# Half-width coupling products in two of four stages of a recurrence, and input gates spread over both

## The chip, the cores and the metric

The kernel runs on one core of a Trainium2 chip. The metric is the device time of one execution in microseconds, as a median over several runs of the same kernel. Beside the runs stands one profiled execution, whose trace records the instructions of each engine: TensorE (PE for matmuls, PEld for loads of the stationary operand), VectorE (DVE), ScalarE (ACT), GpSimd (POOL) and the queue of SyncE (SP).

## The reference

Four layers act on x of shape (8, 256, 512), each added to x. The first two are attention layers (one masked, one modulated by a condition vector). The last two are recurrences over the 256 time steps, for a batch of 8 and 512 features. The oscillator takes one Runge-Kutta step of four stages for each time step:

```python
def _derivative(q, p, drive, coupling, bias):
    i_couple = jnp.tanh(q) @ coupling.T
    dq = q - q ** 3 / 3.0 - p + drive + i_couple + bias
    dp = EPSILON * (q + ALPHA - BETA * p)
    return (dq, dp)

def _rk4_step(q, p, drive, coupling, bias):
    dq1, dp1 = _derivative(q, p, drive, coupling, bias)
    dq2, dp2 = _derivative(q + 0.5 * DT * dq1, p + 0.5 * DT * dp1, drive, coupling, bias)
    dq3, dp3 = _derivative(q + 0.5 * DT * dq2, p + 0.5 * DT * dp2, drive, coupling, bias)
    dq4, dp4 = _derivative(q + DT * dq3, p + DT * dp3, drive, coupling, bias)
    ...
```

Each of the four derivatives needs a product of tanh(q) (8 x 512) with the coupling matrix (512 x 512), and each depends on the one before. The second recurrence is a GRU over the oscillator's result:

```python
def cell(h, x):
    gi = x @ W_ih + b_ih
    gh = h @ W_hh + b_hh
    i_r, i_z, i_n = jnp.split(gi, 3, axis=-1)
    h_r, h_z, h_n = jnp.split(gh, 3, axis=-1)
    r = jax.nn.sigmoid(i_r + h_r)
    z = jax.nn.sigmoid(i_z + h_z)
    n = jnp.tanh(i_n + r * h_n)
    h_new = (1.0 - z) * n + z * h
    return (h_new, h_new)
```

## The kernel before

The attention layers come first (`attention`, lines 25 to 510) and leave the oscillator's drive, transposed, in x2T. Then `scans` runs both recurrences in one loop over the time steps (line 811), written out by hand: the order in the code is the order on each engine. The GRU runs LAG = 7 steps behind the oscillator, since its input gates are made for TS = 4 time steps at once. So from t = 8 to t = 255 every time step holds four oscillator stages s = 0 to 3 and, spread over them, one GRU step.

States are kept transposed: features lie on partitions, four slices and the batch of 8 along the free axis. One stage of the oscillator is this loop:

- `coupling` (line 695) multiplies tanh(q), as stationary operand of 8 columns, with the coupling matrix, as moving operand. The four column blocks j go to the four 32-row strips of one PSUM tile of 128 columns (ic_ps, two of them, used in turn), over four slices k of the contraction. A matmul in fp32 shows in the profile as two records with a load each.
- A VectorE transpose (line 890) brings half of the columns of that tile back to the state's layout, line 891 adds the linear and cubic part (hq) and so gives half of the new q, and `tanh_half` (line 597, on ScalarE) makes the stationary operand of the next stage from it. Then the same for the other half. The first two slices k of the next coupling need the first half of tanh, the last two the second.
- Beside this, ScalarE squares q (line 836), VectorE makes mm (line 847) and hq (line 851) ahead of the transpose, ScalarE scales copies of q (line 679) and GpSimd adds them to the linear parts W of the later stages (line 693). In stage 3, p and the next step's W follow (lines 844 to 846 and `linear_p`).

The GRU step lies between these:

- `gru_products` (line 729) puts 48 products of h and W_hh behind the coupling of its stage: 8 in stage 1, 20 each in stages 2 and 3 (FILL, line 727). All go to one PSUM tile, pg.
- `gru_1` (line 746), in stage 0, transposes pg (line 748), adds the input gates (line 750), and starts the gates r and z on ScalarE and GpSimd. `gru_2` (line 766), in stage 1, makes the argument of n and its tanh, `gru_3` line 773, and `gru_4` (line 775) writes the new h three times into hz (line 778), which the products of stage 1 wait for, and adds it to the output tile on GpSimd (line 785).
- `input_gates` (line 709) multiplies the four finished time steps of a chunk with W_ih, in three parts over three time steps, each behind the coupling of stage 0; `input_gate_out` (line 720) takes the results out in later stages.
- `keep_warm` (line 797) issues matmuls whose result nobody reads, into a PSUM tile of their own, where TensorE would have nothing else.

Of the kernel before, what the change touches and what calls it, by code (L numbers as in the profile page):

```python
# [8 lines left out]
F32 = mybir.dt.float32  # L9
# [5 lines left out]
P = 128  # L15
B, T, D = 8, 256, 512
NJ = D // P
# [511 lines left out]
def scans(ctx, tc, cst, bias, b_ih, b_hh, x2T, out):  # L529
# [49 lines left out]
    psp = ctx.enter_context(tc.tile_pool(name="s_ps", bufs=1, space=PSUM))  # L579

    def rows(j):
        return slice(32 * j, 32 * j + 32)

    cT_sb, wih_sb, whh_sb = cst["weights"]
# [5 lines left out]
    LAG = 2 * TS - 1  # L590
# [9 lines left out]


    q, tT = condS, cst["tanh"]
    ic_ps = [psp.tile([P, P], F32, name=f"ic{i}") for i in range(2)]

    for t in ic_ps:
        nc.vector.memset(t, 0.0)
# [13 lines left out]

    pg_ps = psp.tile([P, P], F32, name="pg")
    gi_ps = psp.tile([P, 3, P], F32, name="gi")
    idle_ps = psp.tile([P, P], F32, name="idle")


    hqs = psp.tile([P, 2, NJ, B], F32, name="hqs")
# [33 lines left out]
    def state3(hz):  # L660
        return hz.rearrange("p k (g x) -> p k g x", x=40)[:, :, :, 0:B]
# [30 lines left out]
        c = scaled(x, [EQ[s][i] for s in range(i + 1, 4)] + [PQ[i]])  # L692
        nc.gpsimd.tensor_tensor(W[:, i + 1 : 5], W[:, i + 1 : 5], c, ALU.add)  # L693

    def coupling(tT, ps):
        for k in range(NJ):
            for j in range(NJ):
                nc.tensor.matmul(  # L698
                    ps[32 * j : 32 * j + B, :],
                    lhsT=tT[k // HM][:, k % HM, :],  # L700
                    rhs=cT_sb[:, k, j * P : (j + 1) * P],
                    start=(k == 0),
                    stop=(k == NJ - 1),
                )


    INPUTS = (((0, 0, 3), (1, 0, 1)), ((1, 1, 3), (2, 0, 2)), ((2, 2, 3), (3, 0, 3)), ())

    def input_gates(c, part):
        for k, g0, g1 in INPUTS[part]:  # L710
            for j in range(NJ):
                nc.tensor.matmul(  # L712
                    gi_ps[rows(j), g0:g1, :],
                    lhsT=x3T[c][:, k, :],
                    rhs=wih_sb[:, k, g0:g1, j * P : (j + 1) * P],
                    start=(k == 0),
                    stop=(k == NJ - 1),
                )

    def input_gate_out(c, g):  # L720
# [8 lines left out]
    def gru_products(tau, s):  # L729
        for k, g0, g1 in FILL[s]:  # L730
            for g in range(g0, g1):
                for j in range(NJ):
                    nc.tensor.matmul(  # L733
                        pg_ps[rows(j), :],
                        lhsT=hzs[tau % 3][:, k, 32 * g : 32 * g + 32],
                        rhs=whh_sb[:, k, g, j * P : (j + 1) * P],
                        start=((k, g) == (0, 0)),
                        stop=((k, g) == (NJ - 1, 2)),
                    )
# [3 lines left out]
    def of_step(tau):  # L743
        return slice(B * (tau % TS), B * (tau % TS) + B)
# [27 lines left out]
    def gru_3():  # L772
        nc.vector.tensor_mul(hm, tn, gru["z1"])  # L773

    def gru_4(tau):

        hz = hzs[(tau + 1) % 3]
        nc.vector.tensor_tensor(  # L778
            state3(hz),
            hm.unsqueeze(2).to_broadcast([P, NJ, 3, B]),  # L780
            gru["zh"].unsqueeze(2).to_broadcast([P, NJ, 3, B]),
            ALU.add,
        )
        x = x3T[tau // TS][:, :, of_step(tau)]
        nc.gpsimd.tensor_tensor(x, x, hz[:, :, 0:B], ALU.add)
# [8 lines left out]
                o[rows(j)].rearrange("p m n -> p (m n)"),  # L794
            )

    def keep_warm(rounds):

        for k in range(rounds):
            for j in range(NJ):  # L800
                nc.tensor.matmul(
                    idle_ps[32 * j : 32 * j + B, :],
                    lhsT=condS[:, k, :],
                    rhs=cT_sb[:, k, j * P : (j + 1) * P],
                    start=True,
                    stop=True,
                )

    with tc.manual_schedule():
        made = []  # L810
        for t in range(T + LAG + 1):
            osc = t < T
            tau = t - LAG
            prod, cell = 0 <= tau < T, 1 <= tau <= T
            inp = TS <= t < T + TS
            c, part = t // TS - 1, t % TS
            if osc:
                if t % TS == 0:
                    x3T[t // TS] = chp.tile([P, NJ, 32], F32, tag="x3T", name=f"x3T_{t // TS}")
                qs = q  # L820
            for s in range(4):
                n = f"{t}_{s}"
                ic = ic_ps[s % 2]

                if osc:
                    coupling(tT, ic)
                if inp and s == 0:
                    input_gates(c, part)
                if t < T + LAG and (not prod or s == 0) and not (inp and s == 0 and INPUTS[part]):
                    keep_warm(2)  # L830
                if not osc and t < T + LAG and s == 3:
                    keep_warm(2)

                if osc:
                    sq, mm, hq = sqmm[:, 0, s % 2], sqmm[:, 1, s % 2], hqs[:, s % 2]
                    nc.scalar.activation(sq, qs, AF.Square, scale=math.sqrt(CUB[s]))  # L836
                if cell and s == 0:
                    gru_1(tau - 1)
                if cell and s == 1:
                    gru_2(tau - 1)  # L840

                if osc:
                    if s == 3:
                        stt(W[:, 4], qs, PQ[3], W[:, 4], ALU.mult, ALU.add)
                        p = st.tile([P, NJ, B], F32, tag="p", name=f"p_{t}")
                        nc.vector.tensor_scalar(p, W[:, 4], CLAMP - OFF, -CLAMP - OFF, ALU.min, ALU.max)  # L846
                    stt(mm, sq, LIN[s], qs, ALU.subtract, ALU.mult)  # L847
                if cell and s == 1:
                    gru_3()
                if osc:  # L850
                    nc.vector.tensor_sub(hq, W[:, s], mm)  # L851
                if cell and s == 1:
                    gru_4(tau - 1)
                if prod:
                    gru_products(tau, s)
                if osc:
                    if s < 3:
                        take(s, qs)
                    if s == 2 and t // US_CH + 1 < T // US_CH:
                        drive(t // US_CH + 1, t % US_CH // NJ, t % NJ)  # L860
                    if t == 0 and s < 3:

                        for i in range(*((0, 5), (5, 10), (10, 16))[s]):
                            drive(0, i // NJ, i % NJ)
                    if 0 < t < TS and s > 0:
                        gru_init(3 * t - 3 + s - 1)
                    if t == TS and s == 1:
                        gru_init(9)
                    if s == 3 and t + 1 < T:
                        W_next = linear_p(t + 1, p)  # L870

                if s == 3:

                    now, made = made, []
                    if cell and (tau - 1) % TS == TS - 1:
                        made.append((tau - 1) // TS)
                    if not osc:
                        now, made = now + made, []
                    for x in now:
                        write_out(x)  # L880
                if inp and (part, s) in ((2, 2), (2, 3), (3, 2)):
                    input_gate_out(c, {(2, 2): 0, (2, 3): 1, (3, 2): 2}[part, s])

                if osc:
                    qn = tmp.tile([P, NJ, B], F32, tag="qn", name=f"qn_{n}", bufs=4)
                    tTn = []
                    for half in range(2):
                        m2 = slice(half * HM, (half + 1) * HM)
                        icT = tmp.tile([P, HM, 32], F32, tag=f"icT{half}", name=f"icT{half}_{n}", bufs=2)
                        nc.vector.transpose(icT.rearrange("p m n -> p (m n)"), ic[:, half * 64 : half * 64 + 64])  # L890
                        stt(qn[:, m2, :], icT[:, :, 0:B], IC[s], hq[:, m2, :], ALU.mult, ALU.add)  # L891
                        if s < 3 or t + 1 < T:

                            tTn.append(tanh_half(qn, half, n))
                    tT = tTn
                    qs = qn
            if osc:
                q = st.tile([P, NJ, B], F32, tag="q", name=f"q_{t}")
                nc.gpsimd.tensor_scalar(q, qs, CLAMP, -CLAMP, ALU.min, ALU.max)
                if t + 1 < T:  # L900
                    W = W_next
                x = x3T[t // TS][:, :, of_step(t)]
                nc.gpsimd.tensor_tensor(x, x2T[:, :, :, t], q, ALU.add)  # L903
# [3 lines left out]
def tile_kernel(  # L907
# [50 lines left out]
    with ExitStack() as s:  # L958
        scans(s, tc, cst, bias, b_ih, b_hh, x2T, out)
# [42 lines left out]
```

## Time and profile before

| | us |
|---|---|
| median of 3 runs | 3043.76 |
| lowest and highest | 3042.32, 3047.22 |
| the profiled execution | 3040.15 |
| its span, first to last instruction | 3038.4 |

The page gives the busy time of each engine over the span, and the costliest groups of instructions; the groups that the change is about are these (line, engine, operation, tiles, shapes, count, then busy us and mean ns of one, then the idle time of the engine before them and what ended most of it):

```profile
PE 2847.2 (94%) x70330; PEld 2070.0 (68%) x70330; DVE 2002.5 (66%) x9090; ACT 1599.9 (53%) x8347; POOL 986.8 (32%) x2905
...
L698 PE MATMUL ic<-cT_sb,tT 128*8 128x128 f32 x32736 | 1088.6, 273 | 82.2 <-ACT tT L598 44.6
L698 PEld LDWEIGHTS ic<-cT_sb,tT 128*8 128x8 f32 x32736 | 758.6, 89 | 344.0 <-ACT tT L598 272.0
L733 PE MATMUL pg<-whh_sb,hz 128*32 128x128 f32 x24576 | 818.5, 274 | 50.7 <-DVE hz L778 17.5
```

Records of one engine overlap: a coupling of 32 records of 273 ns takes 1.06 us from the first start to the last end. A busy time is therefore no sum of costs; what a stage costs is read from the starts in the timeline.

### The profile page before, as it was taken

The page shows a single profiled execution, that of the slowest core. Times are in us where ns is not written, and L with a number is a line of the kernel's source. Part 1 is how long each engine was busy: PE and PEld are TensorE (multiplying, and loading weights), DVE is VectorE, ACT ScalarE, POOL GpSimd, SP SyncE. Part 2 cuts the span into 40 slices and gives each one's busy share as a digit, 9 for nine tenths or more (in the row PEclk, how much of TensorE's full clock was granted, in tenths as well). Part 3 has the DMA queues.
Part 4 walks back from the last instruction along what each step waited for, and adds up shares of the span by engine and source line. Part 5 has one row for each costly group of instructions (what it writes and reads, how often), then busy time and mean ns, then how long its engine had stood idle before and what let it go on. Part 6 is the DMA issues. An engine that isn't in the chain of part 4 may idle for free.

```text
span 3038.4 us, 165918 instructions
## 1 busy us (share of the span) xinstructions
PE 2847.2 (94%) x70330; PEld 2070.0 (68%) x70330; DVE 2002.5 (66%) x9090; ACT 1599.9 (53%) x8347; POOL 986.8 (32%) x2905
## 2 busy tenths in 40 slices
PE   8999999999988899999999999999999999999997
PEld 5455555555545677777777777777777777777775
DVE  4444444544434677777777777777777777777774
ACT  2333433433433566666666666666666666666652
POOL 0021111111221344444444444444444444444442
PEclk8999999999999999999999999999999999999999
DMA  3000000000040000000000000000000000000000
GB/s 129 5 1 1 12 11 1 12 11 1 2 98 2 4 7 6 7 6 6 7 6 7 6 6 7 6 7 6 6 7 6 7 6 6 7 6 7 6 6 7
DMA packets 17759, 35.31 MB, mean 12 GB/s; under 512 B 2144, under 2 KB 10860, under 8 KB 17012
## 3 DMA queue, kind: packets, MB, share of 16 engines
q1 hardware_dynamic: 17012, 24.69, 3.0%
q8 instruction: 550, 9.01, 1.2%
q14 instruction: 197, 1.61, 0.2%
HBM read 20.49 MB, written 4.19 MB: 8 GB/s over the span
## 4 chain that ended last, share of the span: by engine, by line
PE 62%; DVE 26%; ACT 6%; issue 4%; POOL 2%; ACTq 0%; DMA 0%; SPq 0%; POOLq 0%; DVEq 0%
PE pg L733 19%; PE ic L698 17%; PE psqkv L301 5%; DVE icT L890 5%; PE pc L153 5%; DVE qn L891 5%; ACT tT L598 4%; DVE hqs L851 3%; PE s L226 3%; DVE own L748 3%; DVE sqmm L847 2%; PE n L204 2%; DVE v L750 2%; PE psx L401 2%; DVE mxp L209 2%
## 5 line engine op out<-in xcount | busy, mean ns | idle before, releaser
L698 PE MATMUL ic<-cT_sb,tT 128*8 128x128 f32 x32736 | 1088.6, 273 | 82.2 <-ACT tT L598 44.6
L698 PEld LDWEIGHTS ic<-cT_sb,tT 128*8 128x8 f32 x32736 | 758.6, 89 | 344.0 <-ACT tT L598 272.0
L733 PE MATMUL pg<-whh_sb,hz 128*32 128x128 f32 x24576 | 818.5, 274 | 50.7 <-DVE hz L778 17.5
L598 ACT ACTIVATE tT<-qn 128x16 f32<-128x16 f32 x2046 | 440.2, 216 | 646.0 <-DVE qn L891 567.5
L733 PEld LDWEIGHTS pg<-whh_sb,hz 128*32 128x32 f32 x24576 | 667.4, 110 | 125.0 <-DVE hz L778 124.8
L890 DVE STREAM_TRANSPOSE icT<-ic 128x64 f32<-128x64 f32 x2048 | 503.7, 246 | 70.5 <-PE ic L698 64.9
L891 DVE SCALAR_TENSOR_TENSOR qn<-icT,hqs 128x16 f32<-128x16 f32 x2048 | 350.4, 171 | 70.1
L693 POOL TENSOR_TENSOR W<-W,cx 128x128 f32<-128x128 f32 x765 | 297.2, 389 | 256.7 <-ACT cx L679 256.7
L686 POOL TENSOR_TENSOR W<-cx,us 128x128 f32<-128x128 f32 x255 | 117.1, 459 | 446.1 <-ACT cx L679 446.1
L847 DVE SCALAR_TENSOR_TENSOR sqmm<-sqmm,qn 128x32 f32<-128x32 f32 x768 | 153.5, 200 | 152.2 <-ACT sqmm L836 123.1
L209 DVE TENSOR_REDUCE mxp<-n 128x1 f32<-128x512 f32 x256 | 158.7, 683 | 132.0 <-PE n L204 132.0
L851 DVE TENSOR_TENSOR hqs<-W,sqmm 128x32 f32<-128x32 f32 x1020 | 200.1, 196 | 46.1 <-DVE own L773 1.0
L238 ACT ACTIVATE ex<-s 128x512 f32<-128x512 f32 x256 | 132.1, 603 | 157.0 <-PE s L231 157.0
L712 PE MATMUL gi<-wih_sb,x3T 128*32 128x384 f32 (+2 forms) x3072 | 202.4, 379 | 0.5 <-POOL x3T L903 0.5
L324 POOL TENSOR_SCALAR r<-s 128x16 f32<-128x16 f32 x32 | 6.5, 204 | 604.0 <-DVE s L322 603.7
L679 ACT ACTIVATE cx<-qn 128x32 f32<-128x32 f32 x1280 | 200.9, 213 | 0.1
L301 PE MATMUL psqkv<-wqkv_sb,xnT 128*128 128x512 f32 x384 | 181.8, 620 | 0.0
L679 ACT ACTIVATE cx<-p 128x32 f32<-128x32 f32 x1020 | 149.8, 217 | 32.2 <-DVE p L846 1.4
L356 DVE TENSOR_REDUCE mxp<-n 128x2 f32<-128x512 f32 x128 | 79.6, 685 | 107.7 <-PE n L348 107.7
L226 PE MATMUL s<-qm 32*128 32x256 f32 x1024 | 139.4, 406 | 6.8 <-DVE mxp L209 6.8
L679 ACT ACTIVATE cx<-q 128x32 f32<-128x32 f32 x1020 | 145.5, 213 | 0.0
L748 DVE STREAM_TRANSPOSE own<-pg 128x128 f32<-128x128 f32 x256 | 84.9, 332 | 91.3 <-PE pg L733 91.3
(149 smaller groups left out, 3593.5 us busy)
## 6 DMA issues: line engine op xcount, KB each, us to landing
x<-in_x SPq DMA_DIRECT2D x8, 512.0 KB
out<-o SPq DMA_DIRECT2D x256, 16.0 KB
wqkv_sb<-in_L_cond_W_qkv SPq DMA_DIRECT2D x1, 3072.0 KB
wih_sb<-in_L_cond_W_ih SPq DMA_DIRECT2D x4, 768.0 KB
whh_sb<-in_L_cond_W_hh SPq DMA_DIRECT2D x4, 768.0 KB
mk<-in_cond SPq DMA_DIRECT2D x8, 256.0 KB
wemb<-in_L_cond_W_emb SPq DMA_DIRECT2D x4, 512.0 KB
wout_sb<-in_L_cond_W_out SPq DMA_DIRECT2D x1, 1024.0 KB
```

What stands on the lines that cost most here:

```text
L209: nc.vector.tensor_reduce(mxp0[e][:, qc, 32 * h + 1 : 32 * h + 2], ss[h], AX.X, ALU.max)
L226: nc.tensor.matmul(ss[h][:, i, :], lhsT=qm[r : r + 32, e, kc], rhs=qm[r : r + 32, e, qs], start=True, stop=False)
L301: nc.tensor.matmul(ps, lhsT=xnTs[b][:, c, m * P : (m + 1) * P], rhs=wqkv_sb[:, c, part * D : (part + 1) * D], start=(c == 0), stop=(c == N ...
L598: nc.scalar.activation(tT, src[:, half * HM : (half + 1) * HM, :], AF.Tanh)
L679: nc.scalar.activation(c[:, i], x, AF.Copy, scale=f)
L693: nc.gpsimd.tensor_tensor(W[:, i + 1 : 5], W[:, i + 1 : 5], c, ALU.add)
L698: nc.tensor.matmul(ps[32 * j : 32 * j + B, :], lhsT=tT[k // HM][:, k % HM, :], rhs=cT_sb[:, k, j * P : (j + 1) * P], start=(k == 0), stop= ...
L733: nc.tensor.matmul(pg_ps[rows(j), :], lhsT=hzs[tau % 3][:, k, 32 * g : 32 * g + 32], rhs=whh_sb[:, k, g, j * P : (j + 1) * P], start=((k, ...
L847: stt(mm, sq, LIN[s], qs, ALU.subtract, ALU.mult)
L851: nc.vector.tensor_sub(hq, W[:, s], mm)
L890: nc.vector.transpose(icT.rearrange("p m n -> p (m n)"), ic[:, half * 64 : half * 64 + 64])
L891: stt(qn[:, m2, :], icT[:, :, 0:B], IC[s], hq[:, m2, :], ALU.mult, ALU.add)
```

## The change

Four edits, all in `scans`:

1. In stages 0 and 1 a coupling product has 64 columns instead of 128, so that there are 32 matmuls instead of 16. They come in the order AHEAD, (slice k, half): (0,0), (1,0), (0,1), (2,0), (3,0), (1,1), (2,1), (3,1). The halves lie in two PSUM tiles, and three tiles ic_ps are used instead of two (BANKS gives the tile of each stage and half). Stages 2 and 3 keep the whole width and order.
2. `keep_warm` loses its own PSUM tile and writes to that of the three which its stage doesn't use (SPARE).
3. The input gates of each part are divided: most of them stay in stage 0, four matmuls of 128 columns go behind the coupling of stage 1.
4. Where the oscillator runs, `gru_4` and the GRU products of stage 1 are issued between the first transpose of stage 1 and the addition behind it, instead of ahead of that transpose. On VectorE this moves line 778 behind line 890; on GpSimd it moves line 785 behind line 693 of stage 1; on TensorE the order stays.

```diff
-    ic_ps = [psp.tile([P, P], F32, name=f"ic{i}") for i in range(2)]
+    ic_ps = [psp.tile([P, P], F32, name=f"ic{i}") for i in range(3)]
+
+    BANKS = ((0, 1), (2, 0), (1, 1), (2, 2))
+    SPARE = (2, 1, 0, 1)
...
-    idle_ps = psp.tile([P, P], F32, name="idle")
...
-    def coupling(tT, ps):
-        for k in range(NJ):
+    WHOLE = tuple((k, None) for k in range(NJ))
+    AHEAD = ((0, 0), (1, 0), (0, 1), (2, 0), (3, 0), (1, 1), (2, 1), (3, 1))
+
+    def coupling(tT, s):
+        for k, half in AHEAD if s < 2 else WHOLE:
+            n0, n1 = (0, P) if half is None else (64 * half, 64 * half + 64)
+            ps = ic_ps[BANKS[s][half or 0]]
             for j in range(NJ):
                 nc.tensor.matmul(
-                    ps[32 * j : 32 * j + B, :],
+                    ps[32 * j : 32 * j + B, n0:n1],
                     lhsT=tT[k // HM][:, k % HM, :],
-                    rhs=cT_sb[:, k, j * P : (j + 1) * P],
+                    rhs=cT_sb[:, k, j * P + n0 : j * P + n1],
                     start=(k == 0),
                     stop=(k == NJ - 1),
                 )
...
-    INPUTS = (((0, 0, 3), (1, 0, 1)), ((1, 1, 3), (2, 0, 2)), ((2, 2, 3), (3, 0, 3)), ())
-
-    def input_gates(c, part):
-        for k, g0, g1 in INPUTS[part]:
+    INPUTS = (
+        (((0, 0, 3),), ((1, 0, 1),)),
+        (((1, 1, 3), (2, 0, 1)), ((2, 1, 2),)),
+        (((2, 2, 3), (3, 0, 2)), ((3, 2, 3),)),
+        ((), ()),
+    )
+
+    def input_gates(c, units):
+        for k, g0, g1 in units:
...
-    def keep_warm(rounds):
+    def keep_warm(rounds, s):
...
-                    idle_ps[32 * j : 32 * j + B, :],
+                    ic_ps[SPARE[s]][32 * j : 32 * j + B, :],
...
-                if inp and s == 0:
-                    input_gates(c, part)
-                if t < T + LAG and (not prod or s == 0) and not (inp and s == 0 and INPUTS[part]):
-                    keep_warm(2)
+                    coupling(tT, s)
+                units = INPUTS[part][s] if inp and s < 2 else ()
+                input_gates(c, units)
+                if t < T + LAG and (not prod or s == 0) and not units:
+                    keep_warm(2, s)
...
-                if cell and s == 1:
+                if cell and s == 1 and not osc:
                     gru_4(tau - 1)
-                if prod:
+                if prod and not (osc and s == 1):
                     gru_products(tau, s)
...
+                        ic = ic_ps[BANKS[s][half]]
                         nc.vector.transpose(icT.rearrange("p m n -> p (m n)"), ic[:, half * 64 : half * 64 + 64])
+                        if s == 1 and half == 0:
+
+                            if cell:
+                                gru_4(tau - 1)
+                            if prod:
+                                gru_products(tau, s)
                         stt(qn[:, m2, :], icT[:, :, 0:B], IC[s], hq[:, m2, :], ALU.mult, ALU.add)
```

More of the change, by code (lines that the diff above doesn't have):

```diff
@@ L716, in input_gates @@
                     start=(k == 0),
-                    stop=(k == NJ - 1),
+                    stop=((k, g1) == (NJ - 1, 3)),
                 )
@@ L822, in scans @@
                 n = f"{t}_{s}"
-                ic = ic_ps[s % 2]
                 if osc:
-                    coupling(tT, ic)
-                if inp and s == 0:
-                    input_gates(c, part)
-                if t < T + LAG and (not prod or s == 0) and not (inp and s == 0 and INPUTS[part]):
-                    keep_warm(2)
+                    coupling(tT, s)
[3 more added lines that the diff above has]
+                    keep_warm(2, s)
                 if not osc and t < T + LAG and s == 3:
-                    keep_warm(2)
+                    keep_warm(2, s)
                 if osc:
```

## The prediction

> **What bounds the kernel now.** I read the page first. The table of slices shows that the two recurrences fill about two thirds of the span (from 964 us, the first coupling product in the timeline, to 2988 us) at full TensorE clock. The chain that ended last names what decides there:
>
> ```profile
> PE 62%; DVE 26%; ACT 6%; issue 4%; POOL 2%; ACTq 0%; DMA 0%; SPq 0%; POOLq 0%; DVEq 0%
> PE pg L733 19%; PE ic L698 17%; PE psqkv L301 5%; DVE icT L890 5%; PE pc L153 5%; DVE qn L891 5%; ACT tT L598 4%; DVE hqs L851 3%; PE s L226 3%; DVE own L748 3%; DVE sqmm L847 2%; PE n L204 2%; DVE v L750 2%; PE psx L401 2%; DVE mxp L209 2%
> ```
>
> The coupling (L698), the GRU products (L733) and the short loop icT, qn, tT carry it. Then the timeline of one time step, from the last products of stage 3 to the start of stage 2 (start us, length, engine, line, operation, count):
>
> ```profile
> 2006.35 1.27 PE L733 MATMUL pg<-whh_sb,hz 128*32 128x128 f32 x40
> 2007.44 1.06 PE L698 MATMUL ic<-cT_sb,tT 128*8 128x128 f32 x32
> 2007.69 0.33 DVE L748 STREAM_TRANSPOSE own<-pg 128x128 f32<-128x128 f32 x1 [0.27 <-PE pg L733]
> 2008.06 0.26 DVE L750 TENSOR_TENSOR v<-own,gis 128x96 f32<-128x96 f32 x1
> 2008.23 0.19 DVE L847 SCALAR_TENSOR_TENSOR sqmm<-sqmm,q 128x32 f32<-128x32 f32 x1
> 2008.46 0.20 DVE L851 TENSOR_TENSOR hqs<-W,sqmm 128x32 f32<-128x32 f32 x1
> 2008.57 0.25 DVE L890 STREAM_TRANSPOSE icT<-ic 128x64 f32<-128x64 f32 x1
> 2008.85 0.17 DVE L891 SCALAR_TENSOR_TENSOR qn<-icT,hqs 128x16 f32<-128x16 f32 x1
> 2008.94 0.24 DVE L890 STREAM_TRANSPOSE icT<-ic 128x64 f32<-128x64 f32 x1
> 2009.14 0.22 ACT L598 ACTIVATE tT<-qn 128x16 f32<-128x16 f32 x1
> 2009.41 1.06 PE L698 MATMUL ic<-cT_sb,tT 128*8 128x128 f32 x32
> ...
> 2010.17 0.19 DVE L851 TENSOR_TENSOR hqs<-W,sqmm 128x32 f32<-128x32 f32 x1
> 2010.29 0.26 DVE L778 TENSOR_TENSOR hz<-own,zh 128x96 f32<-128x96 f32 x1
> 2010.54 0.25 DVE L890 STREAM_TRANSPOSE icT<-ic 128x64 f32<-128x64 f32 x1
> 2010.61 0.65 PE L733 MATMUL pg<-whh_sb,hz 128*32 128x128 f32 x16
> 2010.82 0.17 DVE L891 SCALAR_TENSOR_TENSOR qn<-icT,hqs 128x16 f32<-128x16 f32 x1
> 2011.11 0.21 ACT L598 ACTIVATE tT<-qn 128x16 f32<-128x16 f32 x1 [0.76 <-DVE qn L891]
> 2011.37 1.06 PE L698 MATMUL ic<-cT_sb,tT 128*8 128x128 f32 x32
> 2012.25 1.27 PE L733 MATMUL pg<-whh_sb,hz 128*32 128x128 f32 x40
> ```
>
> Four things are to be seen. (1) Every stage lasts 1.97 us, from one start of L698 to the next, as a loop of four hops: coupling to first transpose 1.13, transpose to qn 0.28, qn to tanh 0.29, tanh to coupling 0.27. (2) In stages 2 and 3 TensorE is as full as the loop is long: 32 coupling records take 0.88 (2011.37 to 2012.25) and 40 GRU records 1.09 (2006.35 to 2007.44), together 1.97. A round of four records, one for each 32-row strip, is thus 0.109 us. (3) In stage 0, VectorE arrives at the first transpose at the very moment the coupling does: L748 can start only 0.25 after the stage, when stage 3's products have landed, and then 0.37 + 0.17 + 0.23 + 0.11 us of instructions stand in line ahead of L890: 1.13. None of these instructions but L748 has an idle note, and 0.11 is also the gap between L773 and L851, so it is the engine's own pace. (4) In stage 1, L851 starts 0.76 after the stage, and L778 fills the rest.
>
> **What the Trainium skill says.** "TensorE: Matmul & The Clock Gate", section "Wait — 56ns, not 53.3ns?": a stream of matmuls starts every N/2.4 GHz plus about 2.5 ns, but never closer than about 25 ns. The trace agrees on the first (0.109 for 128 fp32 columns, a record being two passes); on the second it shows records of different strips 7 ns apart, so the floor is not one for the whole array, but no record shorter than 128 columns on four strips. The same page, "LDWEIGHTS", prices a load by its columns: 8 here, while the rows show 89 ns. That is latency: the load rows of line 134 (128 columns, 192 ns each, with 8-column matmuls) repeat every 112 ns, so loads overlap what is ahead of them. "PSUM — Partial Sum Buffer", "Terms": a first matmul clears the flags of its whole bank in the strips that it writes; two halves begun apart hence need two banks. "Vector Engine (DVE) Microarchitecture Reference", 3.8: the transpose sustains one element per cycle per lane; the trace below bounds it.
>
> **The change, part by part.**
>
> *Half columns in stages 0 and 1.* Sixteen matmuls (32 records) become 32 (64 records), 32 loads become 64. Estimate for a round of four half records: half of 0.107 plus 2.5 ns, 0.056 us. Eight instructions in 0.056 are 7 ns each; the burst behind a wait shows twelve in 28 ns, so issue should hold. The order asks for three units (6 rounds, 0.336), then needs the second tanh, which comes 0.37 after the first (2008.57 to 2008.94 at the transposes), then two units (4 rounds): the last begins at 0.37 + 0.17 + 0.02 = 0.555. From the last record's start to the transpose there are 0.34 now (0.79 to 1.13), 0.053 less with half the columns: first half ready at 0.84 instead of 1.13. The second half needs 6 rounds more, 1.18, and is wanted 0.37 after the first transpose, at 1.21 or later: the wait that each second transpose now has of its own, with qn, L844 or L767 queued behind it on VectorE, is over before it is reached. TensorE's sum is unchanged but for some 0.03.
>
> *Stage 0.* The order of VectorE is not changed there: L748, L750, L847, L851, then the transpose at 1.13. Stage 3 is not changed either, so L748 keeps its 0.25. **The 0.29 us that the coupling saves is waited for by VectorE: gain 0.** ACT is as tight: its four copies L679 end at about 1.3 us, when the tanh is due.
>
> *Stage 1.* L778 (with the GRU products that wait for it) goes behind the first transpose. This comes at L851 + 0.11 = 0.87 after the stage, later than the coupling's 0.84. Then L778 after the time that a 64-column transpose holds the engine. Not shown alone: at least 67 ns of elements plus the 77 ns that a 32-element instruction has beyond its elements, 0.14; at most 0.21, since a 128-column one (L722, 2004.35) has the next instruction 0.28 behind it, less 0.067. The nearest such pair of the trace is 0.235 apart, 0.17 for 64; I take 0.17. L778 at 1.04; qn 0.174 later (the gap L750 to L847, also 96 elements), at 1.21 instead of 1.41; tanh and coupling 0.55 later: 1.77. But TensorE is in order: hz reaches it 0.31 after L778 starts (2010.29 to 2010.61), at 1.35, and the 16 records (4 rounds) take 0.44: **stage 2 starts at 1.79, not 1.97. Gain 0.18 a step** (0.13 to 0.21 over the two bounds). What is late next is these GRU products.
>
> *Input gates.* The four products of 128 columns moved to stage 1 (0.22) end at 0.93 + 0.22 = 1.15, before hz comes at 1.35: hidden; without that cover, 0.22 a step. Stage 0 keeps 0.64, done at 1.57 of 1.97: hidden. In parts with none, the keep-warm products go to the spare ic bank, whose readers were done before the stage: no wait.
>
> *GpSimd.* L785 now follows stage 1's L693; nobody waits for either within the stage: 0.
>
> *Sums.* Steps 8 to 255 have both recurrences: 248 x 0.18 = 44.6. Steps 0 to 7 have no L748 to L778 ahead of the transposes: about 0.23 + 0.28 each, 4. Against it, 33,000 more TensorE instructions, a quarter more in the recurrences: the timeline has 49 stages some 0.25 us too long, several with "issue" on the loads; a quarter more is 3. Net 45.6. The profiled execution took 3040.15 us, 1.75 around its span of 3038.4, and becomes 2994.5. The median shown is 3.6 higher, 3043.76: **2998**.
>
> **Rivals.**
> A. *The half-width round is priced by a floor* and not by its columns. At 25 ns for each record a round is 0.10; then stage 0 is 16 x 0.10 + 0.64 = 2.24, stage 1 1.6 + 0.22 + 0.44 = 2.26, 0.57 a step more, 141 us: **3185**. It decides from about 0.08 (0.08 x 16 + 0.64 fills stage 0); up to 0.07 nothing changes. For it: nothing so short is in the trace, and 89 ns of load beside 56 of matmul. Against: the 7 ns starts, and line 134. 15%.
> B. *Stage 0 gains too*, were the gaps ahead of its transpose partly a wait for the coupling: 0.28 more a step, 69 us: **2929**. Against it, L851 to L890 is 0.11. 7%.
> C. *The gain is half eaten*: the transpose holds VectorE longer, a round is 0.07 to 0.08, or instruction fetch for the denser stages stalls more often (a 16 KB block of 256 instructions every 4.2 us now, 2.7 at the tightest). Gain 0 to 25 us, about **3030**. 10%.
> The forecast itself has 68%, and its own range is 2985 to 3012.
>
> **Numbers.** 0.2% is 6 us, about what this measurement can tell from none. Faster: forecast, B and half of C, 0.80; same 0.05; slower: A, 0.15. To leave out no more than two in ten, the range goes from 2966, part of the way to B, to 3032, across C.
>
> **What would show it.** Right: starts of the coupling 1.97, about 1.79, 1.97, 1.97 apart; stage 0's L890 still 1.13 behind its coupling with L851 0.11 ahead; stage 1's at 0.87; half-width records in rounds of 0.056. Wrong: rounds of 0.08 or more (A), stage 0 near 1.68 (B), or L778 more than 0.21 behind the transpose (C).

## The result, and the profile after

The forecast was 2998 us; the changed kernel takes **3284.1 us** (median of 4 runs, 3279.6 to 3287.4) against 3043.0 for the kernel before: 1.079 times as long, with a 95% interval from 1.077 to 1.081. Its profiled execution has a span of 3282.2 us.

These lines of the page of the changed kernel answer to those shown of before: the chain that ended last, the groups of the coupling (now L707) and of the GRU products (now L747). The q8 line is the queue that brings TensorE's instructions: its packets times 256 come within 150 of the number of TensorE instructions in both traces. In the kernel before the same line was `q8 instruction: 550, 9.01, 1.2%` (packets, MB, share of the DMA engines' time).

```profile
span 3282.2 us, 200639 instructions
...
q8 instruction: 685, 11.22, 1.4%
...
PE 79%; issue 8%; DVE 7%; ACT 5%; POOL 2%; DMA 0%; ACTq 0%; SPq 0%; POOLq 0%; DVEq 0%
...
L707 PE MATMUL ic<-cT_sb,tT 128*8 128x64 f32 x49088 | 1266.4, 237 | 165.9 <-issue 121.7
L707 PEld LDWEIGHTS ic<-cT_sb,tT 128*8 128x8 f32 x49088 | 964.4, 89 | 373.5 <-issue 195.1
L747 PE MATMUL pg<-whh_sb,hz 128*32 128x128 f32 x24576 | 931.8, 274 | 67.4 <-issue 45.4
```

VectorE, which had 26% of the chain, has 7%. TensorE has 79% of it instead of 62%, and "issue" 8% of the span against 4%. "Issue" is time in which an engine waits for nothing that the profile shows. Before, TensorE's loads for the coupling stood idle mostly for the tanh (272 us of 344); now they stand idle mostly for nothing visible (195 us of 373).

One such wait in the timeline of the changed kernel (start us, length, engine, line, operation, count, idle time before it and its releaser):

```profile
2199.37 1.10 PE L707 MATMUL ic<-cT_sb,tT 128*8 128x64 f32 x60
2201.19 0.23 PE L707 MATMUL ic<-cT_sb,tT 128*8 128x64 f32 x2 [0.72 <-issue]
2201.20 0.52 PE L726 MATMUL gi<-wih_sb,x3T 128*32 128x384 f32 x2
2201.24 0.23 PE L707 MATMUL ic<-cT_sb,tT 128*8 128x64 f32 x2
...
2201.51 0.25 DVE L904 STREAM_TRANSPOSE icT<-ic 128x64 f32<-128x64 f32 x1 [0.57 <-PE ic L707]
```

The coupling of stage 0 has 64 records. Sixty start in one stretch, then TensorE stops in the middle of a product whose operands are all there, for 0.9 us from one record's start to the next, and the last four come after it. The second transpose of the stage waits for them.

Where these gaps lie tells their cause. I counted TensorE's records (each load and each product is one instruction) and the transfers of its instruction queue in the trace, between 1100 and 2900 us. A transfer brings 16,384 bytes; there are 426 of them for 109,248 TensorE instructions before, so it is a block of 256 instructions. A gap here is the time from one record's start to the next.

```
                               before     changed
TensorE instructions per us     60.7       69.2
blocks, mean spacing us          4.22       3.70
blocks, least spacing us         3.26       3.28
gaps over 0.14 us with no wait   329        555
  their sum us                   81         292
```

In the changed kernel more than half of the gaps are exactly 256 instructions behind the one before. The middle half of them end within 1.34 to 1.51 us of the end of a block's transfer. Before, most stand at fixed places of the step, 8, 472, 480 or 944 instructions apart, where input gates of 256 and 384 columns are streamed, and have no fixed distance to a transfer. So the changed kernel waits for its own instructions: a block comes each 3.70 us, 14.4 ns for an instruction. A step with both recurrences has 616 of them (384 for the coupling, 192 for the GRU products, 32 for the input gates, 8 for keep-warm products) where it had 480; 616 x 14.4 ns is 8.9 us. Measured over steps 60 to 239 it is 8.91 us, where before it was 7.91. That the two agree proves nothing yet, since in any kernel blocks come on average as fast as their instructions are used. The evidence in this trace is where the gaps lie; the rate of 14.4 ns is put to the test by kernels with other counts.

### The profile page after: what moved, and what is told of

It reads as the page before. It is cut to its first block, busy times and chain, and to the rows that moved or that the text cites. A ratio compares the mean times of both kernels' runs of the same rounds, so it can differ in the third digit from the quotient of the medians.

```text
span 3282.2 us, 200639 instructions
## 1 busy us (share of the span) xinstructions
PE 2961.1 (90%) x87690; PEld 2249.9 (69%) x87690; DVE 1966.6 (60%) x9091; ACT 1597.7 (49%) x8347; POOL 993.5 (30%) x2905
## 4 chain that ended last, share of the span: by engine, by line
PE 79%; issue 8%; DVE 7%; ACT 5%; POOL 2%; DMA 0%; ACTq 0%; SPq 0%; POOLq 0%; DVEq 0%
PE ic L707 27%; PE pg L747 23%; PE psqkv L301 5%; PE pc L153 5%; PE gi L726 4%; PE s L226 3%; PE n L204 2%; PE psx L401 2%; DVE mxp L209 2%; PE s L231 1%; ACT cx L681 1%; DVE own L762 1%; PE s L371 1%; POOL r L325 1%; ACT tT L598 1%
## 5 line engine op out<-in xcount | busy, mean ns | idle before, releaser
L707 PE MATMUL ic<-cT_sb,tT 128*8 128x64 f32 x49088 | 1266.4, 237 | 165.9 <-issue 121.7
L707 PEld LDWEIGHTS ic<-cT_sb,tT 128*8 128x8 f32 x49088 | 964.4, 89 | 373.5 <-issue 195.1
L747 PE MATMUL pg<-whh_sb,hz 128*32 128x128 f32 x24576 | 931.8, 274 | 67.4 <-issue 45.4
L747 PEld LDWEIGHTS pg<-whh_sb,hz 128*32 128x32 f32 x24576 | 743.6, 110 | 147.3 <-issue 83.9
L726 PE MATMUL gi<-wih_sb,x3T 128*32 128x128 f32 (+2 forms) x4096 | 273.4, 327 | 23.5 <-issue 23.1
L864 DVE TENSOR_TENSOR hqs<-W,sqmm 128x32 f32<-128x32 f32 x1020 | 199.8, 196 | 46.8 <-DVE sqmm L860 1.4
L726 PEld LDWEIGHTS gi<-wih_sb,x3T 128*32 128x32 f32 x4096 | 133.4, 110 | 37.8 <-issue 31.9
```

Source lines behind the costliest of these rows:

```text
L707: nc.tensor.matmul(ps[32 * j : 32 * j + B, n0:n1], lhsT=tT[k // HM][:, k % HM, :], rhs=cT_sb[:, k, j * P + n0 : j * P + n1], start=(k == 0 ...
L726: nc.tensor.matmul(gi_ps[rows(j), g0:g1, :], lhsT=x3T[c][:, k, :], rhs=wih_sb[:, k, g0:g1, j * P : (j + 1) * P], start=(k == 0), stop=((k, ...
L747: nc.tensor.matmul(pg_ps[rows(j), :], lhsT=hzs[tau % 3][:, k, 32 * g : 32 * g + 32], rhs=whh_sb[:, k, g, j * P : (j + 1) * P], start=((k, ...
```

## The experiments

My theory after the result was that of instruction fetch: a step lasts the longer of its loop and of 14.4 ns for each TensorE instruction. The rivals were that half-width products are slow themselves (the forecast's rival A), that VectorE's new order costs the time, and that the input gates in stage 1 do.

**The count alone.** The kernel before with small products, whose result nobody reads, where TensorE had been idle:

```diff
+    def tiny(count):
+        for i in range(count):
+            j = i % NJ
+            nc.tensor.matmul(
+                idle_ps[32 * j : 32 * j + B, 0:8],
+                lhsT=condS[:, 0, :],
+                rhs=cT_sb[:, 0, j * P : j * P + 8],
+                start=True,
+                stop=True,
+            )
...
+                if osc and s < 2:
+                    tiny(16)
```

> The kernel before, with 32 matmuls of 8 columns more in each oscillator step (16 behind the input gates of stage 0, 16 behind the coupling of stage 1, results never read): 128 more TensorE instructions a step, 608 instead of 480, placed where TensorE had been idle 0.2 and 0.3 us. Theory of instruction fetch (256 instructions each 3.70 us, 14.4 ns each): 608 x 14.4 ns = 8.79 us a step instead of 7.87, some 235 us more, about 3275 us, with issue gaps every 256 instructions. Rival, that the half-width products or their order cost the time: their 16 short rounds fit the idle time but for 0.1 us at most, so under 3070 us.

Measured: 3279.1 us, 1.077 (1.075 to 1.078). No half-width product, no changed order, and yet the changed kernel's time. Its page shows the same sign, and its timeline a gap in the middle of the small products (L813), which wait for nobody:

```profile
PE 78%; DVE 10%; issue 6%; ACT 4%; POOL 2%; ACTq 0%; DMA 0%; SPq 0%; POOLq 0%; DVEq 0%
...
L813 PEld LDWEIGHTS idle<-cT_sb,condS 128*8 128x8 f32 x16384 | 251.7, 88 | 78.5 <-issue 65.7
```

```profile
2205.97 0.26 PE L813 MATMUL idle<-cT_sb,condS 128*8 128x8 f32 x12
2206.64 0.28 PE L813 MATMUL idle<-cT_sb,condS 128*8 128x8 f32 x18 [0.41 <-issue]
```

The blocks stand 3.73 us apart here. The small products take hardly any time of their own: the shortest tenth of stages 0 and 1 in this trace last up to 1.99 and 1.97 us, against 1.97 before. So the count by itself takes about as much as the whole change did. With half as many, `tiny(8)`:

> The kernel before with 16 matmuls of 8 columns more a step (8 in stage 0, 8 in stage 1): 544 TensorE instructions a step, as many as with half-width products in stage 1 alone. Fetch allows 7.86 us, the loop needs 7.87, and late blocks cost some: 3050 to 3090 us, and about as much above the loop's own time as the half-width version of the same count lies above 7.69 us a step. Rival without fetch: 3044 us.

Measured: 3077.0 us, 1.011 (1.009 to 1.012). At 544 instructions the mean need just meets the rate, and the kernel is 33 us slower all the same. That the uneven need for blocks within a step costs them is my reading and isn't shown. The second half of the expectation failed: the half-width kernel of this count, below, lies 52 us or more above its own, shorter loop, not 33.

**Half-width products in stage 1 alone.** The changed kernel with the input gates of before, and

```diff
-    BANKS = ((0, 1), (2, 0), (1, 1), (2, 2))
-    SPARE = (2, 1, 0, 1)
+    BANKS = ((0, 0), (2, 1), (0, 0), (2, 2))
+    SPARE = (1, 0, 1, 1)
...
-        for k, half in AHEAD if s < 2 else WHOLE:
+        for k, half in AHEAD if s == 1 else WHOLE:
```

> The changed kernel with half-width products in stage 1 alone, the input gates as in the kernel before, line 778's move kept: 544 TensorE instructions a step. Fetch theory: 544 x 14.4 ns = 7.86 us a step, the time of before, so 3040 to 3065 us, although the undisturbed stages give 7.69. Rival, that half-width products themselves lose time: half of the loss stays, about 3160 us. Rival, that the prediction's sum is right but for stage 0: 3000 us.

Measured: 3052.4 us, 1.003 (1.002 to 1.004), as fetch has it and far from half of the loss. The same with one slice of input gates in each part, which saves 16 instructions more:

```diff
+    INPUTS = (
+        (((0, 0, 3),), ()),
+        (((1, 0, 3),), ()),
+        (((2, 0, 3),), ()),
+        (((3, 0, 3),), ()),
+    )
...
+                if inp and (part, s) in ((3, 1), (3, 2), (3, 3)):
+                    input_gate_out(c, {(3, 1): 0, (3, 2): 1, (3, 3): 2}[part, s])
```

> As the run with half-width products in stage 1 alone, but one whole slice of input gates in each of the four parts (4 matmuls of 384 columns) and so no keep-warm products: 528 TensorE instructions a step. Fetch theory: 7.63 us a step would be enough, less than the 7.69 of the undisturbed stages, so the gain of stage 1 shows in part: 3000 to 3025 us, faster than both kernels. Rival of half-width products: 3150 us or more.

Measured: **3025.5 us, 0.993 (0.992 to 0.995)**, 19 us faster than the kernel before. (One of the six runs took 4739.9 us; the other five lie between 3018.6 and 3029.4.) Its timeline shows an undisturbed stage 1, and with it what the half-width products of this stage are worth when the instructions arrive:

```profile
2200.87 1.11 PE L707 MATMUL ic<-cT_sb,tT 128*8 128x64 f32 x64 [0.26 <-ACT tT L598]
2201.63 0.20 DVE L864 TENSOR_TENSOR hqs<-W,sqmm 128x32 f32<-128x32 f32 x1
2201.73 0.24 DVE L904 STREAM_TRANSPOSE icT<-ic 128x64 f32<-128x64 f32 x1
2201.90 0.22 DVE L792 TENSOR_TENSOR hz<-own,zh 128x96 f32<-128x96 f32 x1
2202.04 0.15 DVE L911 SCALAR_TENSOR_TENSOR qn<-icT,hqs 128x16 f32<-128x16 f32 x1
...
2202.17 0.64 PE L747 MATMUL pg<-whh_sb,hz 128*32 128x128 f32 x16 [0.19 <-DVE hz L792]
...
2202.63 1.06 PE L707 MATMUL ic<-cT_sb,tT 128*8 128x128 f32 x32
```

Stage 1 begins at 2200.87, its first transpose comes 0.86 later, 0.10 behind L864; hz (L792) 0.17 behind that, the GRU products at 1.30, and the next coupling's first product at 1.76 instead of 1.97. Over steps 60 to 239 the medians of the four stages, by the first load of each, are 1.967, 1.713, 2.016 and 1.966: stages 1 and 2 together take 3.73 instead of 3.93. But the mean step is 7.83, not the 7.66 of the medians. Some 0.06 of the difference comes from taking out the input gates, which in every fourth step makes stage 1 last 1.91 and stage 0 of the next step 2.03; 0.10 is left for late blocks and other delays, where the kernel before has 0.04.

**The order alone.** The kernel before with the fourth edit and nothing else (for the diff, see the change).

> The kernel before with the fourth edit alone (line 778 and the GRU products of stage 1 behind the first transpose of that stage); the number of instructions is as before. The transpose still comes at 1.13, hz 0.4 us later than it did, so the GRU products end after the next tanh: some 0.05 us a step, about 3055 us. Rival, that the new order of VectorE is what costs the time: 3200 us or more.

Measured: 3058.2 us, 1.005 (1.003 to 1.006). The order costs 14 us where the coupling isn't early; as a cause of the 241 it is out.

**Undoing the input gates.** The changed kernel with the input gates of before.

> The changed kernel with the input gates as in the kernel before (all behind stage 0, 24 instead of 32 TensorE instructions a step): 608 a step instead of 616. Fetch theory: 8 x 14.4 ns = 0.12 us a step less, about 3255 us. Rival, that the time does not go by the number of instructions: 3284 us, or more, since stage 0 is fuller.

Measured: 3273.6 us, 1.076 (1.073 to 1.079). The sign is right, but 11 us less is not 29, and the interval overlaps that of the changed kernel (1.077 to 1.081): by itself this run says nothing for fetch. It does rule out the moved input gates as the main cause, since 230 us of the 241 stay without them. In its profiled execution the steps 8 to 254 are 21 us shorter in all than in the changed kernel's, and the recurrences begin 9 us later (step 1 starts at 980.6 us instead of 971.6, ahead of any input gate): part of what the count saves is hidden by that. The changed kernel with one slice in each part (the INPUTS shown above), 24 instructions less:

> The changed kernel, half-width products in stages 0 and 1, with one whole slice of input gates in each of the four parts and no keep-warm products: 592 TensorE instructions a step. Fetch theory: 8.55 us a step, 24 x 14.4 ns = 0.35 less than the changed kernel, about 3200 us. Rival, that the half-width products themselves cost the time: 3270 us or more.

Measured: 3217.2 us, 1.057 (1.055 to 1.059), 67 us less for 24 x 248 = 5,952 instructions, 11 ns each. The time goes by the count here too, at a somewhat lower price than 14.4. In its trace the blocks stand 3.73 us apart instead of 3.70, so that each of the 592 instructions takes 14.6 ns. Why the blocks come less densely, I haven't settled.

**What the lean inputs cost.** The kernel before with one slice in each part:

> The kernel before with one whole slice of input gates in each of the four parts and no keep-warm products: 464 TensorE instructions a step instead of 480. Fetch alone would allow 6.70 us a step, the loop needs 7.87: the time stays but for the odd late blocks, 3032 to 3044 us. It tells what of the lean run's gain comes from the inputs and what from the half-width products of stage 1. Rival, that the instructions saved are worth 14.4 ns each here too: 57 us less, 2987 us.

Measured: 3053.2 us, 1.003 (1.002 to 1.004): slower. Fewer instructions are worth nothing where the loop sets the time, but I had not expected a loss. In its trace stages 2 and 3 last 1.97 us on average as ever, stage 1 2.01: there the transpose of input gates now stood, once in four steps, ahead of the coupling's, and that stage lasts 2.09 (median). Stage 0 of the next step lasts 2.03. The next run takes the results out where the kernel before does, with 20 matmuls a chunk and no keep-warm products:

```diff
+    INPUTS = (
+        (((0, 0, 3),), ()),
+        (((1, 0, 3),), ((2, 0, 1),)),
+        (((2, 1, 3), (3, 0, 3)), ()),
+        ((), ()),
+    )
...
-                if t < T + LAG and (not prod or s == 0) and not (inp and s == 0 and INPUTS[part]):
+                if t < T + LAG and not prod and not units:
```

> The kernel before with the same input gates and without keep-warm products: 468 TensorE instructions a step, the loop's 7.87 us stays: 3032 to 3044 us. Rival, that a clock or an idle TensorE made the lean version of before slower and not its transposes in stage 1: about 3053 us again.

Measured: 3042.9 us, 1.000 (0.999 to 1.001). So neither a clock nor an idle TensorE made the lean version slower, since keep-warm products are missing here too. Both long stages are back at 1.97, which fits the place of the transposes; the run also spreads the input gates otherwise, so the place alone isn't shown. And 12 instructions less a step are worth nothing where fetch isn't the bound. With these inputs and half-width products in stage 1:

> Half-width products in stage 1 alone, no keep-warm products while the GRU runs, and the input gates in 20 matmuls a chunk, their results taken out where the kernel before does: 532 TensorE instructions a step, of which fetch allows one in 7.69 us; the undisturbed stages need 7.66. No transpose of input gates stands in stage 1 any more, which cost the lean kernels about 10 us. Fetch theory with that: 3005 to 3020 us, below the first lean version. If the transposes in stage 1 were not what the lean versions lost: 3025 us or more.

Measured: 3037.2 us, 0.998 (0.997 to 0.999): a miss. The kernel should have lost the transposes' 10 us and instead is 12 us slower than the first lean version, with 4 instructions more and less evenly spread. Its trace does show the long stages gone: with the median of each stage a step would last 7.67. The mean is 7.91, so the delays on top cost 0.24 a step, where the first lean version had 0.10. The last run leaves the first lean version's products as they are and only moves the transpose from stage 1 to stage 3:

```diff
-                if inp and (part, s) in ((3, 1), (3, 2), (3, 3)):
-                    input_gate_out(c, {(3, 1): 0, (3, 2): 1, (3, 3): 2}[part, s])
+                if inp and (part, s) in ((3, 2), (3, 3)):
+                    for g in {2: (0,), 3: (1, 2)}[s]:
+                        input_gate_out(c, g)
```

> The first lean version with half-width products in stage 1, with the one transpose of input gates that stood in stage 1 put into stage 3, where VectorE waits 0.46 us: 528 TensorE instructions a step, spread evenly over the four parts. Stage 1 loses its 0.2 us every fourth step no more, stage 3 loses 0.1: 3010 to 3022 us. If fetch alone sets the time by now: 3025 us, unchanged.

Measured: 3026.8 us, 0.994 (0.992 to 0.995), unchanged. That is what the expectation had for the case that fetch alone sets the time, but the trace shows another reason. Stage 1 did lose its delay: in every fourth step its median is 1.71 instead of 1.91. But stage 0 of the step after it now lasts 2.21 instead of 2.03. These lines show why (L738 adds the bias to the input gates that were taken out, L920 makes the new q):

```profile
2094.58 0.87 POOL L738 TENSOR_TENSOR gis<-git,gbias 128x128 f32<-128x128 f32 x2
2094.97 0.77 PEld L707 LDWEIGHTS ic<-cT_sb,tT 128*8 128x8 f32 x32
2095.54 0.21 POOL L920 TENSOR_SCALAR q<-qn 128x32 f32<-128x32 f32 x1
2095.78 0.20 ACT L849 ACTIVATE sqmm<-q 128x32 f32<-128x32 f32 x1 [0.50 <-POOL q L920]
2096.36 0.24 DVE L905 STREAM_TRANSPOSE icT<-ic 128x64 f32<-128x64 f32 x1
```

Two transposes in stage 3 mean two additions on GpSimd, and q waits behind them. The square of q, and with it the transpose, comes late: 1.39 us after the coupling instead of 1.12. The delay was moved from VectorE to GpSimd, not removed, so this run doesn't tell how near the lean kernels are to the limit of fetch. Their blocks come 3.80 us apart on average, where the changed kernel gets one each 3.70.

## Why the prediction was wrong

- **The half-width round of 0.056 us**: right. The trace of the changed kernel has rounds of four records 56 ns apart wherever its instructions are there. Rival A had the right side and more than half of the loss (141 us of 241), but not the cause: no round is priced by a floor. That it came nearest is luck. The Trainium skill's 25 ns ("TensorE: Matmul & The Clock Gate", "Wait — 56ns, not 53.3ns?") doesn't bind here: a round of four takes 56 ns, 14 for a record. (The loads of line 134, read as repeating every 112 ns, do so in 43 of 63 cases and are mostly 213 ns apart in the others; the round didn't hang on it.)
- **Stage 0 gains nothing**: right. These lines of the changed kernel show a stage 0 that no gap disturbs; the transpose is 1.12 behind the coupling and 0.10 behind L864:

```profile
2208.17 1.13 PE L707 MATMUL ic<-cT_sb,tT 128*8 128x64 f32 x62
...
2209.19 0.20 DVE L864 TENSOR_TENSOR hqs<-W,sqmm 128x32 f32<-128x32 f32 x1
2209.29 0.24 DVE L904 STREAM_TRANSPOSE icT<-ic 128x64 f32<-128x64 f32 x1
```

- **Stage 1 gains 0.18 a step**: right as a mechanism, 0.20 in the medians of the lean version. In the changed kernel it is seen only in part: from step 8 to step 254 its stage 1 lasts 1.83 or more in all steps but one, and whether the input gates moved there are hidden stays open. In the lean version the transpose at 0.87, L792 0.17 behind it and the GRU products as the last to hold stage 2 are as forecast; qn comes 0.31 behind the transpose, not 0.34. (The 67 ns for 64 elements in that working are about 64 by the gaps that it reads itself, 0.11 us for 32 elements and 0.174 for 96; the lower bound of 0.14 stays.)
- **The step that failed is the last term of the sums**: "Against it, 33,000 more TensorE instructions, a quarter more in the recurrences: [...] a quarter more is 3". There are 34,720 more, and they cost some 289 us instead of 3 (3284 less the 2995 that the other terms, taken as right, leave of 3044). The term took instruction fetch for a source of stray late blocks that grows with the count. It is a rate with a limit, and the change went past it. Behind the term stands a reading that failed with it: from twelve instructions in 28 ns behind a wait the forecast concluded that "issue should hold". Such a burst says nothing of the mean rate, which in the changed kernel is one instruction each 14.4 ns. Rival C named the block and 2.7 us as the tightest spacing, but didn't ask whether blocks can come that close.

That comparison was to be had before: the forecast's own step, 616 instructions in 7.69 us, asks for a block every 3.20 us. In the trace of before no two blocks are nearer than 3.26. The forecast thus asked each block to come faster than the fastest one of 426. It would have been a warning and no more: TensorE never starts 256 instructions in less than 3.40 us in that trace, so it doesn't show what fetch can do at most, and a block each 3.26 us would make the step 7.84 us, the time of before. The 3.70 us that blocks take where TensorE waits for them show only in a run that goes past the limit.

## What to carry to other kernels

Count the instructions of each engine per unit of the loop, not only their durations, whenever a change splits instructions: divide by the forecast's time and compare with the block spacing that the trace shows at its densest. A forecast that asks for more than any trace has shown needs a run that adds the instructions alone, as the first experiment does. Where fp32 matmuls are issued as two loads and two products each, a split of N columns in two makes eight instructions of four, for about the same time of the array. And apply a split only where the wait that it shortens ends last: stage 0 paid 64 instructions a step for nothing, and leaving it whole turned a loss of 241 us into a gain of 19, together with 24 instructions saved at the input gates and keep-warm products.

## What the runs showed of the hardware

- Where TensorE waits for blocks of 256 instructions, it gets one each 3.70 to 3.73 us on average (the changed kernel, its two versions with other input gates, and the kernel with 32 small products), 69 instructions per us. In the changed kernel the transfer itself takes 1.1 us of that; TensorE goes on 1.4 us after its end, and the next transfer starts 1.1 to 1.2 us later. The three about add up to the spacing, which looks like one block asked for at a time, when the one before it is begun; the runs show the intervals, not the mechanism.
- The Trainium skill ("Runtime: NRT & Kernel Launch", "Instruction fetch mechanics") describes the 16 KiB blocks of 256 instructions, as the trace has them, and says that fetch is hidden because the sequencer dispatches slower than the blocks arrive. Here it isn't hidden: TensorE takes bursts of loads and products 1 to 7 ns apart and then stands, in the changed kernel up to 1.7 us.
- Near the limit, time is lost before the mean need reaches it: 544 instructions in a loop of 7.87 us need a block each 3.70 us, as much as there is, and cost 33 us. In the first lean version, 528 in 7.66, late blocks can account for at most some 0.10 us of the 0.17 that a step loses.
